# A graph network's edge sums: bf16 parts in threes on 96 rows, or float32r parts in pairs on two 64-row halves

## The chip, the cores and the metric

The kernel runs on one core of a Trainium2 chip. A core has a matrix engine (TensorE, PE in the profile, with its weight loads as PEld), a vector engine (VectorE, DVE), a scalar engine (ScalarE, ACT), a general engine (GpSimd, POOL) and a queue that issues most of the DMA transfers (SyncE, SP). Matrix products go to PSUM, a small memory of eight banks; VectorE and ScalarE read them there. The metric is the time of one execution on the device, in microseconds, as the median of several runs.

## The reference

There are 128 graphs of 128 nodes with 64 features, and an adjacency matrix for each. Layer 0 passes messages over edges, layer 1 is one aggregation.

```python
# layer 0, h = max(layernorm(x), 0)
mask = (adj > 0.0)
xj_proj = h @ W1a
diff = h[:, :, None, :] - h[:, None, :, :]
hid = relu(xj_proj[:, :, None, :] + diff @ W1b + b1)     # (b, j, k, 192)
hm = einsum('bjkh,bjk->bjh', hid, mask)
deg = sum(mask, axis=-1)
x = x + hm @ W2 + deg[..., None] * b2
# layer 1, h = max(layernorm(x), 0)
x = x + einsum('bnm,bmf->bnf', adj, h) @ W.T
```

Only the entries of `mask` that are one add to `hm`. A node has about 16 neighbours among 128 nodes, so most of the (j, k) pairs need not be computed.

## The kernel before

For a node j the hidden vector of an edge to k is relu(A[j] - C[k]), where A = h(W1a + W1b) + b1 and C = h W1b. A and C are 192 wide: units 0 to 127 (C0 = 128) go one way, units 128 to 191 (C1 = 64) another.

**Slots.** The kernel takes the graphs in 32 groups (NG) of four (G = 4). The 128 neighbours k of a node fall into four quarters (Q = 4) of 32. Within a quarter each edge gets a rank, and the first six (D = 6) edges of each quarter go into slots. `pre_rank` (line 442) makes the ranks by a product of a triangular matrix with the mask; `pre_slots` (line 455) compares the ranks with a constant tile `rks` and so makes a one-hot tensor `S`, in bf16. A product of the one-hot tensor with the C values of that quarter picks the neighbour's C for each slot, a product of an identity with the A values adds A[j]. The result lies in PSUM with hidden units on partitions and slot times node on columns. Edges past the sixth of a quarter go an extra way (the `pre_edge_...` functions, `edge_x`, the one-hot tensors `R` and `S2`), and `edge_sum` and `edge_sum1` add what slots and extra edges have in common.

**Exact parts.** TensorE multiplies bf16 in one pass. To keep float32 accuracy the A and C values (`ca`) are split into three bf16 parts in `pre_proj` (line 538): ScalarE copies the product out as the first part, VectorE subtracts it (`rest`), ScalarE makes the second part, GpSimd the third. With 32 nodes of a quarter in three parts, 96 rows (K3) of the array are in use. `pre_stack` (line 607) copies the parts into this layout (`k3`) by 12 transfers, and `pre_slots` copies `S` three times below itself for each quarter (`S3`) by another 12. All of these stand on SP's queue.

**Jobs.** A group has 24 jobs (class `Job`, line 811). A job takes one PSUM tile of two banks; each bank holds one quarter, six slots, 64 nodes (384 columns). A kind-0 job fills all 128 partitions with units 0 to 127 of one graph: two products of 384 columns with `S3` and four of 192 columns with the identity `id3`. A kind-1 job fills two halves of 64 partitions with units 128 to 191 of two graphs: four products of 384 and eight of 192 columns. A kind-0 tile is drained by one VectorE reduction of absolute values into `hm0`; a kind-1 tile by a ScalarE relu into `T` and adds on GpSimd. There are 16 kind-0 and 8 kind-1 jobs in a group, and three tiles of this kind, which `pre_proj` uses too.

**Order.** TensorE's order is the order of the program (`mm` and `tp`, lines 180 to 184). After each job the loop at line 977 runs what three tables name for that step: `AHEAD` prepares the next group, `OWN` belongs to this one, `BEHIND` finishes the group before. The other engines' instructions are placed by the scheduler once the first group has been prepared (`Engine.held`, line 972). The first group has its own preparation: `first_ranks` and `first_slots` make the ranks and slots on tripled rows directly, so that no copies of `S` are needed.

Of the kernel before, what the change touches and what calls it, by code (L numbers as in the profile page):

```python
# [8 lines left out]
F32 = mybir.dt.float32  # L9
BF16 = mybir.dt.bfloat16  # L10
I32 = mybir.dt.int32
# [139 lines left out]
def kernel(  # L151
# [50 lines left out]

    vec, act, pool, sp = (Engine(e) for e in (nc.vector, nc.scalar, nc.gpsimd, nc.sync))
# [15 lines left out]
    K3 = 3 * QN  # L219
# [8 lines left out]
    with ExitStack() as main:  # L228
# [41 lines left out]
        triq = const.tile([P, P], BF16, tag="triq", name="triq")  # L270
        vec.memset(triq, 0.0)
# [3 lines left out]

        triq3 = tmp.tile([P, Q, 3, QN], BF16, tag="u0", name="triq3", bufs=1)
        for part in range(3):
            vec.tensor_copy(
                triq3[:, :, part], triq.rearrange("p (q j) -> p q j", q=Q)
            )  # L280
# [5 lines left out]

        rks = const.tile([P, D, G * N], BF16, tag="rks", name="rks")
        for i in range(D):
            pool.memset(rks[:, i], float(i) + BIG)

        mident = const.tile([P, P], F32, tag="mident", name="mident")
        identb = const.tile([P, P], BF16, tag="identb", name="identb")

        id32 = const.tile([P, QN], F32, tag="id32", name="id32")
        id3 = const.tile([P, QN], BF16, tag="id3", name="id3")
# [3 lines left out]
        def constants():  # L299
            vec.tensor_scalar(mident, ident, -1.0, None, ALU.mult)  # L300
            vec.tensor_copy(identb, ident)
# [3 lines left out]
            vec.tensor_copy(id3, id32)  # L305
# [15 lines left out]

        def weight_loads():
            act.dma_start(w2a, W2[0:C0, :])
            act.dma_start(b1c, b1[0:C0].unsqueeze(1))
            act.dma_start(bias[:, 0:H], b1.unsqueeze(0).to_broadcast([P, H]))
            act.dma_start(b2s, b2.unsqueeze(0).to_broadcast([P, O]))
            for p in range(2):
                s = slice(p * F, (p + 1) * F)
                sp.dma_start(w1[s], W1.rearrange("(t f) h -> f t h", t=2))
# [16 lines left out]
        def weights_b():  # L346
# [3 lines left out]
            pw = mtile("pw")  # L350
            tp(pw[:, 0:P], wab[:, 0:C0], ident)
            vec.tensor_tensor(bias[:, H : H + O], pb[:, 0:O], b2s, ALU.add)
            vec.tensor_scalar(wp[:, 0:H], w1[:, 1], -1.0, None, ALU.mult)
            vec.tensor_copy(wT, pw[:, 0:P])
# [27 lines left out]
        groups: dict[int, dict] = {}  # L382

# [31 lines left out]
        def load(g):  # L415
# [3 lines left out]
            d["adj"] = loads.tile([P, G, N], F32, tag="adj", name=f"adj{g}")  # L419
            sp.dma_start(d["adj"], adj[g * G : (g + 1) * G].rearrange("b j k -> j b k"))  # L420

        def pre_adj(g):
# [8 lines left out]
            d["maskT"] = grp.tile([P, G, N], BF16, tag="maskT", name=f"maskT{g}")  # L431
# [10 lines left out]
        def pre_rank(g):  # L442
# [5 lines left out]
            d["qs"] = grp.tile([P, G, N], BF16, tag="qs", name=f"qs{g}")  # L448
            qf = d["qs"].rearrange("k b j -> k (b j)")
            act.activation(qf, pq, AF.Copy)  # L450

            d["ov"] = grp.tile([P, G, N], BF16, tag="ov", name=f"ov{g}")
            vec.tensor_scalar(d["ov"], d["qs"], float(D) + BIG, None, ALU.is_ge)

        def pre_slots(g, first, last):

            d = groups[g]
            if first == 0:
                d["S"] = one.tile([P, D, G * N], BF16, tag="S", name=f"S{g}")
            n = last - first  # L460
            vec.tensor_tensor(
                d["S"][:, first:last], bc(d["qs"].rearrange("k b j -> k (b j)"), n, 1),
                rks[:, first:last], ALU.is_equal,
            )
            if last < D:
                return
            d["S3"] = grp.tile([K3, Q, D, G * N], BF16, tag="S3", name=f"S3{g}")
            for q in range(Q):
                for part in range(3):
                    sp.dma_start(  # L470
                        d["S3"][part * QN : (part + 1) * QN, q],
                        d["S"][q * QN : (q + 1) * QN],
                    )

        def first_ranks(g, qp):

            d = groups[g]
            pk = gtile(f"pk{g}_{qp}")
            if qp == 0:
                d["q3"] = tmp.tile([K3, Q, G * N], BF16, tag="T", name=f"q3{g}", bufs=3)  # L480
            for i in range(2):
# [545 lines left out]
```

## Time and profile before

| what | us |
|---|---|
| median of three runs | 1012.33 (1009.71 to 1015.56) |
| the profiled execution, its span | 1013.2 |
| busy: PE, DVE, ACT, POOL | 963.8, 799.7, 704.1, 765.9 |
| first job begins | 26.2 |
| groups 1 to 30 | 65.5 to 971.2 |
| last job ends, about | 996 |

The page of the profile has one execution, and this one took as long as the runs. Engines are in rows by their short names. A row of the groups gives line, engine, operation, what is written and read, shapes and count, then busy time, the mean duration of one in ns, and the idle time before such instructions with what ended it. Lines 181 and 184 are the helpers that record each product and transpose, and line 198 the helper that records each instruction of the other engines, so the names of the tiles tell which one is meant. The 40 digits of PEclk are the granted clock of TensorE in tenths, for 40 equal slices of the span.

### The profile page before, as it was taken

What the parts mean: (1) busy time and instruction counts of PE and PEld (TensorE: products, weight loads), DVE (VectorE), ACT (ScalarE), POOL (GpSimd) and SP (SyncE); (2) the same over time, 40 slices, a digit from 0 to 9 for tenths busy, and PEclk for the clock granted to TensorE, in tenths of its full rate; (3) what the DMA queues carried; (4) which work ended last, traced back from release to release, by engine and by line L of the source; (5) the groups of instructions that cost most, each with busy time, mean ns of one, the idle gap of its engine ahead of it and who ended that gap; (6) DMA issues with size and microseconds to landing.
All of it is one profiled execution on the core that took longest, in us unless ns stands there. A gap on an engine that the chain in (4) does not pass through costs nothing.

```text
span 1013.2 us, 27270 instructions
## 1 busy us (share of the span) xinstructions
PE 963.8 (95%) x10314; PEld 721.6 (71%) x10314; DVE 799.7 (79%) x1769; ACT 704.1 (69%) x1732; POOL 765.9 (76%) x1134
## 2 busy tenths in 40 slices
PE   3899999999999999999999999999999999999996
PEld 2577777777777777777777777777767777777774
DVE  7767888777888877788877788877787877788863
ACT  5557876677777667777667787667786667787652
POOL 3278777787877777877778877777877778877783
PEclk9599999999999999999999999999999999999998
DMA  3526655556755556766555766545765555765420
GB/s 83 133 68 162 147 135 130 123 124 154 161 136 134 122 120 140 163 136 138 126 123 129 162 144 136 131 112 128 162 140 133 127 120 132 162 147 119 110 67 14
DMA packets 88296, 129.94 MB, mean 128 GB/s; under 512 B 47200, under 2 KB 63968, under 8 KB 88160
## 3 DMA queue, kind: packets, MB, share of 16 engines
q1 hardware_dynamic: 87584, 127.98, 55.2%
q8 instruction: 83, 1.36, 0.5%
q14 instruction: 53, 0.43, 0.1%
q10 hardware_dynamic: 576, 0.16, 0.1%
HBM read 13.01 MB, written 4.19 MB: 17 GB/s over the span
## 4 chain that ended last, share of the span: by engine, by line
PE 45%; DVE 25%; ACT 14%; DMA 5%; POOL 4%; issue 3%; SPq 2%; DVEq 1%; POOLq 0%; ACTq 0%
PE g L181 24%; DVE hm L198 9%; PE pe L181 8%; DVE S L198 8%; DMA k<-ca 4%; ACT ca L198 3%; PE px L181 3%; DVE u L198 3%; ACT et L198 3%; POOL T L198 3%; SPq L198 2%; PE pp L181 2%; PE py L181 2%; ACT h L198 2%; ACT T L198 2%
## 5 line engine op out<-in xcount | busy, mean ns | idle before, releaser
L198 POOL TENSOR_TENSOR T<-T 128x192 f32<-128x192 f32 (+2 forms) x768 | 543.6, 714 | 139.0 <-ACT T L198 99.1
L181 PEld LDWEIGHTS <-k 96*128 96x128 bf16 (+1 forms) x6144 | 412.4, 104 | 208.5 <-issue 87.4
L198 DVE TENSOR_REDUCE hm<-g 128x64 f32<-128x768 f32 x512 | 472.1, 948 | 110.4 <-PE g L181 108.6
L181 PE MATMUL g<-S,k 96*128 96x384 bf16 (+1 forms) x2048 | 392.1, 333 | 29.2 <-DMA k<-ca 14.3
L181 PE MATMUL g<-id,k 96*128 96x192 bf16 (+1 forms) x4096 | 384.1, 248 | 0.0
L198 ACT ACTIVATE T<-g 128x768 f32<-128x768 f32 x256 | 209.8, 821 | 48.5 <-PE g L181 48.5
L198 POOL TENSOR_TENSOR ca<-rest,ca 128x384 bf16<-128x384 f32 x126 | 114.0, 924 | 82.3 <-ACT ca L198 72.0
L198 ACT ACTIVATE ca<-pp 128x768 bf16<-128x768 f32 x64 | 51.3, 802 | 63.9 <-PE pp L181 63.9
L198 DVE TENSOR_TENSOR S<-qs,rks 128x1024 bf16<-128x1024 bf16 x93 | 86.9, 962 | 0.1
L198 ACT ACTIVATE hT<-ph 128x256 f32<-128x256 f32 x32 | 12.3, 383 | 104.0 <-PE ph L184 104.0
L181 PE MATMUL pe<-RT,X 128*64 128x128 f32 (+1 forms) x512 | 74.9, 285 | 0.0
L181 PE MATMUL pe<-mident,z 128*64 128x128 f32 (+1 forms) x512 | 68.8, 274 | 0.0
L181 PE MATMUL pp<-wp,hT 64*128 64x448 f32 x256 | 68.7, 614 | 0.0
L198 ACT ACTIVATE z<-pp,ns 128x128 f32<-128x128 f32 (+1 forms) x256 | 65.7, 347 | 0.0
L198 ACT ACTIVATE ca<-rest 128x768 bf16<-128x768 f32 x64 | 55.2, 863 | 11.6 <-DVE rest L198 11.6
L198 DVE TENSOR_TENSOR rest<-pp,ca 128x768 f32<-128x768 f32 x64 | 60.7, 948 | 3.2 <-ACT ca L198 3.1
L198 DVE TENSOR_SCALAR maskT<-adjT 128x512 bf16<-128x512 f32 x32 | 17.2, 538 | 52.7 <-PE pe L181 52.7
L198 ACT ACTIVATE et<-et,half 128x128 f32<-128x128 f32 x128 | 56.8, 449 | 0.0
L181 PEld LDWEIGHTS pe<-mident,z 128*64 128x64 f32 (+1 forms) x512 | 53.8, 164 | 0.0
L181 PEld LDWEIGHTS pe<-RT,X 128*64 128x64 f32 (+1 forms) x512 | 52.8, 164 | 0.1
L181 PE MATMUL px<-ca,S 128*128 128x192 bf16 x384 | 52.7, 246 | 0.0
L181 PE MATMUL px<-ca,R 128*128 128x192 bf16 x384 | 52.6, 246 | 0.0
(128 smaller groups left out, 1263.1 us busy)
## 6 DMA issues: line engine op xcount, KB each, us to landing
S<-S SPq DMA_DIRECT2D x372, 192.0 KB, 4.0
k<-ca SPq DMA_DIRECT2D x384, 96.0 KB, 2.2
adj<-in_adj_dram SPq DMA_DIRECT2D x32, 256.0 KB, 3.0
x<-in_x_dram SPq DMA_DIRECT2D x32, 128.0 KB, 2.7
out_dram<-ot SPq DMA_DIRECT2D x32, 128.0 KB, 2.2
w<-in_L_gnn_W_dram SPq DMA_DIRECT2D x2, 96.0 KB, 5.1
bias<-in_L_gnn_b_dram ACTq DMA_DIRECT2D x1, 96.0 KB, 4.6
w2a<-in_L_gnn_W_dram ACTq DMA_DIRECT2D x1, 32.0 KB, 2.2
```

The costliest lines, as they stand in the source:

```text
L181: return tc.keep_in_program_order(nc.tensor.matmul(*args, **kw))
L198: ins = f(*args, **kw)
```

## The change

The A and C values are split into two parts of float32r, a 4-byte type[...], instead of three of bf16. The first part is a ScalarE copy, the second a VectorE subtraction straight from PSUM. 32 nodes in two parts are 64 rows, so that two quarters lie on the two halves of the array: bank 0 of a slot tile is fed by rows 0 to 63, bank 1 by rows 64 to 127. The kind-1 jobs now write all 128 partitions at once; zeros beside the C values keep the halves apart. The ranks are made by two more products on doubled rows, so `S` is made in its final layout by six instructions with a constant, and is copied nowhere. `rks` and the functions for the first group's ranks go away. The mask, the one-hot tensors and the identity become float32r as well. The bodies of `pre_proj` and `pre_stack` follow; the tables are moved to later steps in places, `edge_sum` is cut in two, and some VectorE instructions are now held in the order of the program (`keep`).

```diff
+    def keep(ins):
+        return ins if Engine.held else tc.keep_in_program_order(ins)
...
-            d["adj"] = loads.tile([P, G, N], F32, tag="adj", name=f"adj{g}")
+            d["adj"] = loads.tile([P, G, N], F32, tag="adj", name=f"adj{g}", bufs=1)
...
-            d["maskT"] = grp.tile([P, G, N], BF16, tag="maskT", name=f"maskT{g}")
+            d["maskT"] = grp.tile([P, G, N], F32R, tag="maskT", name=f"maskT{g}")
...
+            pk = gtile(f"pk{g}")
+            for c in range(2):
+                mm(
+                    pk[:, c], trist[:, c], d["maskT"].rearrange("k b j -> k (b j)"),
+                    start=True, stop=True,
+                )
+            d["q2"] = tmp.tile([P, 2, G * N], BF16, tag="q2", name=f"q2{g}", bufs=1)
+            act.activation(d["q2"], pk, AF.Copy)
...
-            vec.tensor_tensor(
-                d["S"][:, first:last], bc(d["qs"].rearrange("k b j -> k (b j)"), n, 1),
-                rks[:, first:last], ALU.is_equal,
-            )
-            if last < D:
-                return
-            d["S3"] = grp.tile([K3, Q, D, G * N], BF16, tag="S3", name=f"S3{g}")
-            for q in range(Q):
-                for part in range(3):
-                    sp.dma_start(
-                        d["S3"][part * QN : (part + 1) * QN, q],
-                        d["S"][q * QN : (q + 1) * QN],
-                    )
+                d["S"] = grp.tile([P, 2, D, G * N], F32R, tag="S", name=f"S{g}")
+            for i in range(first, last):
+                keep(vec.tensor_scalar(
+                    d["S"][:, :, i], d["q2"], float(i) + BIG, None, ALU.is_equal
+                ))
...
-            act.activation(parts[0], x, AF.Copy)
-            rest = tmp.tile([P, 2, 2, H], F32, tag="rest", name=f"rest{g}_{r}")
+            for t in range(2):
+                act.activation(part(0, t), x[:, :, t], AF.Copy)
...
             zs()
             es()
-            vec.tensor_tensor(rest, x, parts[0], ALU.subtract)
-            second()
-            third(pool)
+            for t in range(2):
+                keep(vec.tensor_tensor(part(1, t), x[:, :, t], part(0, t), ALU.subtract))
...
-                sp.dma_start(
-                    d["k3"][part * QN : (part + 1) * QN, q],
-                    d["ca"][q * QN : (q + 1) * QN, part],
-                )
+            for h in range(2):
+                for part in range(2):
+                    for i in range(2):
+                        sp.dma_start(kc[rows(2 * i + part), h], ca[rows(2 * h + i), part])
+                for w in range(2 * h, 2 * h + 2):
+                    for part in range(2):
+                        for i in range(2):
+                            sp.dma_start(ka[rows(2 * i + part), w], ar[rows(w), part])
...
+                if self.kind == 0:
+                    nodes, centre = [(b, p * (H + 2 * C1))], p * (H + C1)
                 else:
+                    nodes, centre = [(r, LOWER), (2 + r, UPPER)], C0
+                for n, (src, a) in enumerate(nodes):
+                    j0 = src * N + jh * JH
+                    for i, rows in enumerate(TILE):
                         mm(
+                            self.gt[:, i, 0:ND].rearrange("h (d j) -> h d j", d=D),
+                            d["kc"][rows, qp, r, a : a + P],
+                            d["S"][rows, qp, :, j0 : j0 + JH],
+                            start=n == 0, stop=False, skip_group_check=True,
                         )
                 for w in range(2):
+                    for i, rows in enumerate(TILE):
+                        o = self.gt[:, i, 0:ND].rearrange("h (d j) -> h d j", d=D)
+                        mm(
+                            o[:, :, w * QN : (w + 1) * QN],
+                            d["ka"][rows, 2 * jh + w, r, centre : centre + P],
+                            bc(id32r[rows], D, 1),
+                            start=False, stop=w == 1, skip_group_check=True,
+                        )
...
-            0: (pre_adj,),
-            2: (pre_norm, pre_hT,),
-            3: (pre_rank, lambda g: pre_slots(g, 0, 2),),
-            4: (lambda g: pre_slots(g, 2, 4),),
-            5: (pre_count,),
-            6: (lambda g: pre_slots(g, 4, D),),
-            7: (lambda g: pre_proj(g, 0),),
-            9: (pre_edge_a,),
-            12: (lambda g: pre_proj(g, 1), pre_stack,),
+            3: (pre_rank,),
+            4: (pre_count, lambda g: pre_slots(g, 0, 1)),
+            6: (lambda g: pre_slots(g, 1, 2),),
+            7: (lambda g: pre_proj(g, 0),),
+            8: (lambda g: pre_slots(g, 2, 3), pre_edge_a),
+            10: (lambda g: pre_slots(g, 3, 4),),
+            11: (lambda g: pre_proj(g, 1), pre_stack),
+            12: (lambda g: pre_slots(g, 4, 5),),
+            14: (lambda g: pre_slots(g, 5, D),),
...
-            1: (edge_sum,),
-            4: (edge_sum1,),
-            8: (post0,),
-            10: (post1,),
+            1: (lambda g: edge_sum(g, 0),),
+            2: (lambda g: edge_sum(g, 1),),
+            5: (edge_sum1,),
+            9: (post0,),
+            13: (post1,),
```

`TILE` is the two row ranges 0 to 63 and 64 to 127, `trist` the triangular matrix with each quarter's columns twice, `kc` the stacked C values with zeros beside them, `ka` the stacked A values. In `edge_x`, `edge_sum` and the extra edges' products the parts are two instead of three.

## The prediction

> **What bounds the kernel now.** I read the page's first part, then the busy time of each engine over one group of the middle of the run, then TensorE's instructions in order of time there, then the groups of VectorE that the change touches.
>
> ```profile
> PE 963.8 (95%) x10314; PEld 721.6 (71%) x10314; DVE 799.7 (79%) x1769; ACT 704.1 (69%) x1732; POOL 765.9 (76%) x1134
> PEclk9599999999999999999999999999999999999998
> 486.60:516.50 29.90, 29.49 (x325) 22.22 (x323) 24.40 (x54) 21.68 (x55) 23.75 (x36) 1.00 0.60 136
> ```
>
> The last line is one group of four nodesets: length, then busy us of PE, weight loads, DVE, ACT, POOL, then the granted clock. PE is busy 29.49 of 29.90. A matmul's record is longer than its turn, so I check by starts:
>
> ```profile
> 499.75 0.66 PE g L181 x6
> 501.59 1.54 PE g L181 x18
> 505.64 0.99 PE px L181 x12
> 486.61 0.60 PE L184 MATMUL pt<-ident,adj 128*128 128x128 f32 x4
> 487.05 0.64 PE L181 MATMUL g<-S,k 96*128 96x384 bf16 x2
> 488.50 0.44 PE L181 MATMUL pe<-RT,X 128*128 128x128 f32 x2
> 488.77 0.39 PE L181 MATMUL pe<-mident,z 128*128 128x128 f32 x2
> 489.00 0.33 PE L181 MATMUL pe<-maskT,ca 128*128 128x128 bf16 x3
> 489.17 0.44 PE L181 MATMUL pe<-RT,X 128*128 128x128 f32 x2
> 503.05 1.02 PE L181 MATMUL pp<-wp,hT 64*128 64x448 f32 x4
> 503.91 0.28 PE L181 MATMUL pp<-biasp,oneb 64*128 64x256 bf16 x2
> 504.17 0.32 PE L181 MATMUL g<-S,k 96*128 96x384 bf16 x1
> ```
>
> The first three are from the chain of waits (start, us, what): a kind-0 job (6 matmuls, 1536 columns) takes 0.66 us, 0.43 ns a column; 12+6 matmuls take 1.54, so a kind-1 job with its switch of array shape about 0.8. The rest is PE's timeline. Three bf16 matmuls of 128 columns take 0.17 us from 489.00 to 489.17 (0.055 each); a plain f32 one of two records 0.23 to 0.27; an f32 transpose, one record, 0.11. PE has no gap to give: it paces the 30 middle groups, which begin at 65.5 us and every 30.2 us to 971.2. The rest is 65.5 us of start with group 0, 24.8 of last group (971.2 to 996.0, PE 24.78 busy) and 17.2 of tail: 65.5+30x30.2+24.8+17.2 = 1013.5, the profiled execution's 1013.2. The median of the runs, 1012.33, is the same within 0.1%.
>
> **The change, TensorE.** Per group there are 16 kind-0 and 8 kind-1 jobs. The trace has no float32r, so its rate is bounded: below by bf16 (0.43 ns a column), above by plain f32 (0.25 us for 128 columns, 1.95 ns), between them the transpose (0.86). The Trainium skill, "FP8 and Floating Point Precision", TensorE Precision Notes, has four passes for true FP32 and a truncating read for reduced precision; that points to one pass, the lower end, which I take. That the two 64-row halves run side by side is seen: the four pp records (two instructions of 448 f32 columns) take 503.91-503.05 = 0.86 us, where one after the other they would take 2x448x1.95 = 1.75.
> - Kind 0: one S pair (384 columns, 0.163) and two id pairs (2x192, 0.081 each): 0.325 instead of 0.65; 16 x -0.325 = -5.2 us.
> - Kind 1: two S pairs, two id pairs: 0.49 instead of 0.78; 8 x -0.29 = -2.3.
> - Three parts become two: px 16 instead of 24 matmuls of 0.083: -0.66; ca with maskT 8 instead of 12 of 0.055: -0.22. The doubled ranks add two of 512 columns: +0.43.
> - Against it, drains. "TensorEngine Tiling (Array Packing)", Key Properties: a change of tiling mode drains the array. Row: the bias pair starts at 503.91 and needs 0.11, the next S matmul, full shape, starts at 504.17: 0.15 idle. Now that is paid around kind 1 and pp; after it, all jobs are half-height and about 16 pieces between them (pt, edge sums, px, py ...) full. I take 0.2 for going and coming, 16 x 0.2 = +3.2. Without the rule it would be nothing.
>
> Sum -4.75: PE needs about 25.4 us a group. A second rule speaks against it: "TensorE: Matmul & The Clock Gate", LDWEIGHTS and Weight-path perf modes: fast weight load is not for FP32, and a load takes columns/1.2, 107 ns for 128. Row: a load of k (128 columns, bf16) reads 98 ns, of the f32 transposes 143, of the f32 products 191. If a 128-column float32r load holds its half for 107 ns, each matmul of 192 or 128 columns costs 0.107: jobs +1.25, px +0.4, maskT +0.4, prt and pgq +0.4, counts +0.2, so 28.1 us. Range 25.4 to 28.1, either below today's 30.2.
>
> **VectorE becomes the pace.** It is busy 24.40 us a group now.
>
> ```profile
> L198 DVE TENSOR_REDUCE hm<-g 128x64 f32<-128x768 f32 x512 | 472.1, 948 | 110.4 <-PE g L181 108.6
> L198 DVE TENSOR_TENSOR S<-qs,rks 128x1024 bf16<-128x1024 bf16 x93 | 86.9, 962 | 0.1
> L198 DVE TENSOR_TENSOR rest<-pp,ca 128x768 f32<-128x768 f32 x64 | 60.7, 948 | 3.2 <-ACT ca L198 3.1
> L198 DVE TENSOR_SCALAR maskT<-adjT 128x512 bf16<-128x512 f32 x32 | 17.2, 538 | 52.7 <-PE pe L181 52.7
> ```
>
> - The 16 reductions stay: 15 us.
> - S: out go three of 962 ns (86.9/31 = -2.8). In come six tensor_scalars of 1024 elements from bf16 to float32r. Nearest row: maskT, also of mixed types and from SBUF, 512 elements, shortest 409 and median 478 ns; two elements a cycle are 0.27 of them, some 0.15 is fixed (ov, 512 bf16, 281 ns): 1024 take 0.53+0.16 = 0.69. S and maskT today also wait: S reads 0.68 when free and 1.48 behind a long POOL add. POOL is busy 70% of the time; I add 0.25 each, half of a mean POOL instruction: 6x0.94 = +5.6. Ends: 4.1 without waits, 7.3 at one element a cycle (6x1.22).
> - rest: two of 948 become four of half size (0.40+0.15): +0.3.
> 27.5 us busy. Some waits cannot be hidden: now S2 waits 0.66 us a group for pgq (21.1 over 32), and ov, dn, ns each wait on the other engines once; I add 1.5: **29.0 us**; with PE at 25 to 28 beside it and three PSUM slots shared by jobs, pp and the new pk, 29.2.
>
> **The others** are covered by VectorE's 29: ACT 21.68 - 2x0.86 (second parts) - 2x0.80 + 4x0.49 (half-size copies, between its 0.42 for 256 and 0.60 for 512) + 1.0 (doubled ranks, 1010 ns in group 0's row) = 21.3. POOL loses four of 0.92: 20.1. SP issues 24 copies a group as now (12 S and 12 k; then 8 kc and 16 ka) at 0.6: 14.2 us. They start when the second pre_proj's remainders are done, some 16.5 us into the group; the first twelve serve the next group's first job and land at 16.5+7.1+2.2 = 26, three us before it; the last are needed six jobs later. Behind them on SP stand only the output and loads for later groups. The one adj buffer is refilled a group ahead. If that cover of 3 us goes, each us late is 30 us in all.
>
> **Start and end.** First job 26.2 now. It loses 8.2 us of S work on VectorE (four of 2.0) and the third parts (1.7), gains six S (4.1), and waits for 12 copies instead of 6 (+3.6): about 27. Group 0 took 39.3, half of it at half clock; with jobs half as long on PE, 37. Together 64. The last group falls from 24.8 to 20.5, where POOL's 19 us of adds and slot sums bound it; tail 17.2. Sum 64 + 30x29.2 + 20.5 + 17.2 = **978 us**.
>
> **Rivals.**
> 1. VectorE costs more: S at one element a cycle or behind every POOL add (+1.7), remainders waiting behind ACT with reductions queued behind them. 31 us a group: 102+930 = 1032. For it: S has been seen at 1.48. Against: maskT's 409.
> 2. The other side: float32r streams at the transposes' rate (0.86 ns a column), or the two halves do not overlap, so the change doesn't do what it says. Kind 0 stays 0.65, kind 1 0.98 (+1.6), drains +3.2, px +0.6, ranks +1.1, the 128-column ones +0.7: PE 37.4, about 1220 us. It turns slower than before as soon as a job's pair takes over 1.5 times its bf16 time. For it: every 4-byte record here takes two cycles or more a column. Against: the precision notes, and pp's halves side by side.
> 3. Only the narrow ones (192 and 128 columns) fall to plain f32's 1.95 ns: kind 0 0.9, kind 1 1.07, px +3.9: PE 45, about 1430.
>
> **Numbers.** My forecast 0.62, its own range 945 to 1020; rival 1 0.11, rival 2 0.17, rival 3 0.10. 0.5% is about what a measurement here can tell from no change. Of my forecast three quarters lie under 1007, and some near it, since PE at 28 and VectorE at 29 may trip over each other: faster 0.62x0.75+0.01 = 0.47; same 0.08; slower 0.45. The range leaves out rival 3 and the best ends: 946 to 1235.
>
> **What would show it.** Right: g<-S records near 326 ns with pairs starting together, PE's busy share falling well below 95% or its idle time naming DVE; S rows of 0.7 to 1.0 us; hm idle time no longer on PE g; groups 29 us apart. Wrong: id pairs more than 0.12 apart (rival 2 or 3), PE still at 95%; S rows above 1.2; PE waiting for ka or adj.

## The result, and the profile after

The changed kernel takes 1515.2 us (median of four runs, 1496.27 to 1539.7) where the kernel before takes 1013.94 (1009.71 to 1015.86). Two of the four ran slower, at a granted clock of 0.70 for 0.73, and the comparison leaves them out: with 1496.27 and 1502.73 us the changed kernel takes 1.481 times as long, 95% interval 1.472 to 1.490. The prediction was 978 us, with a range from 946 to 1235; the result lies outside. The profile below is that of the run of 1502.73 us.

First the page of the changed kernel: busy times, the granted clock in 40 slices, and the groups of jobs, slots and remainders.

```profile
PE 1300.6 (87%) x8967; PEld 1054.0 (70%) x8967; DVE 871.8 (58%) x1927; ACT 699.4 (47%) x1762; POOL 670.5 (45%) x1004
PEclk9888979777778667765777667765677657776688
L182 PE MATMUL g<-S,kc 64*128 64x384 f32 x2048 | 476.4, 504 | 160.3 <-DVE ar L199 71.8
L182 PE MATMUL g<-id32r,ka 64*128 64x192 f32 x3072 | 358.1, 317 | 2.8 <-DMA ka<-ar 2.6
L199 DVE TENSOR_REDUCE hm<-g 128x64 f32<-128x768 f32 x512 | 485.6, 951 | 267.8 <-PE g L182 264.9
L199 DVE TENSOR_SCALAR S<-q 128x1024 fp32r<-128x1024 bf16 x192 | 157.5, 822 | 0.0
L199 DVE TENSOR_TENSOR ca<-pp,ca 128x384 fp32r<-128x384 f32 x64 | 35.7, 558 | 116.6 <-ACT e L199 116.6
```

The second line is what the reader should see first. Before, its digits were nearly all 9; now most are 5 to 8. The mean granted clock of the profiled execution is 0.729 (0.980 before). VectorE, which the prediction made the pace, is busy 58%.

One group in the middle (it begins at 700.7 us and the next at 748.5), in stretches of 5 us: the stretch, its length, then busy us of PE, weight loads, VectorE, ScalarE and GpSimd with counts, then the granted clock and the transfers.

```profile
700.00:705.00 5.00, 5.00 (x27) 4.33 (x27) 2.44 (x3) 0.60 (x1) 3.13 (x6) 0.50 0.19 52
705.00:710.00 5.00, 5.00 (x26) 4.38 (x26) 1.54 (x3) 0.21 (x1) 0.00 (x0) 0.50 0.00 0
710.00:715.00 5.00, 5.00 (x49) 4.10 (x47) 2.76 (x8) 3.15 (x5) 1.08 (x1) 0.83 0.00 0
715.00:720.00 5.00, 4.11 (x43) 2.73 (x40) 3.79 (x8) 3.02 (x12) 4.17 (x7) 1.00 0.02 3
725.00:730.00 5.00, 2.69 (x21) 2.38 (x20) 3.79 (x6) 1.18 (x6) 3.34 (x6) 0.87 0.53 119
740.00:745.00 5.00, 5.00 (x27) 4.08 (x27) 2.34 (x3) 1.19 (x2) 3.33 (x7) 0.50 0.51 116
```

From 700 to 710 TensorE is busy all the time, yet at half clock: 26 or 27 matmuls in 5 us, 49 in the stretch in which the clock comes back. It falls again after the line at 725. The clock changes at steps of 3.413 us, and most groups have settled at exactly 14 of these, 47.8 us: nine at half clock, five at full. The wait that precedes the fall, in TensorE's order of time:

```profile
724.64 0.44 PE L185 MATMUL pty<-ident,ys 128*128 128x128 f32 x2
727.38 0.44 PE L182 MATMUL g<-S,kc 64*128 64x384 f32 x2 [2.31 <-DVE ar L199]
726.21 0.56 DVE L199 TENSOR_TENSOR ca<-pp,ca 128x384 fp32r<-128x384 f32 x1 [2.87 <-ACT e L199]
```

A job waits 2.31 us for its PSUM tile. It is the tile that the projection `pp` held, and the last to read it is the new subtraction `ar`. This one stands on VectorE behind `ca`, and `ca` waits 2.87 us for ScalarE's `e`, though it needs nothing of `e`.

To place the loss, I cut each group in two by the first matmul of `po` (slot 20) and that of `pp` (slot 7 of the next group). Stretch A runs from `po` to `pp`, with slots 21 to 23 and 0 to 7; stretch B from `pp` to `po`, with slots 8 to 20. One group of the kernel before (A, then B), and one of the changed kernel (B, then A):

```profile
572.02:586.61 14.59, 14.55 (x175) 11.85 (x173) 11.99 (x19) 8.43 (x17) 11.48 (x18) 1.00 0.37 89
586.61:601.91 15.30, 14.81 (x151) 10.44 (x151) 12.62 (x37) 13.43 (x38) 12.45 (x19) 1.00 0.82 184
```

```profile
716.07:740.06 23.99, 18.78 (x137) 14.36 (x133) 17.11 (x42) 14.90 (x45) 11.27 (x17) 0.76 0.41 92
740.06:763.86 23.80, 23.80 (x151) 20.29 (x150) 9.84 (x18) 6.94 (x10) 9.71 (x16) 0.59 0.15 36
```

The medians over 27 groups are A 14.86 and B 15.20 before, A 23.80 and B 23.99 after. Both stretches lose about 9 us, but they look different: in A TensorE is never idle and the clock is 0.59; in B TensorE has 5 us without work, and VectorE's busy time has grown by 4.5 us.

### The profile page after: what moved, and what is told of

Its sections match the earlier page's. It is cut to its first block, busy times and chain, and to the rows that moved or that the text cites. A ratio compares the mean times of both kernels' runs of the same rounds, so it can differ in the third digit from the quotient of the medians.

```text
span 1501.0 us, 25137 instructions
## 1 busy us (share of the span) xinstructions
PE 1300.6 (87%) x8967; PEld 1054.0 (70%) x8967; DVE 871.8 (58%) x1927; ACT 699.4 (47%) x1762; POOL 670.5 (45%) x1004
## 4 chain that ended last, share of the span: by engine, by line
PE 56%; DVE 21%; ACT 18%; issue 3%; DMA 1%; POOL 1%; ACTq 0%; DVEq 0%; SPq 0%; POOLq 0%
PE g L182 23%; PE pe L182 12%; DVE hm L199 9%; ACT h L199 5%; DVE S L199 5%; PE pp L182 5%; ACT z L199 4%; ACT T L199 3%; PE po L182 2%; DVE ar L199 2%; PE prt L182 2%; PE pt L185 2%; PE pgq L182 2%; ACT ar L199 2%; PE pj L182 2%
## 5 line engine op out<-in xcount | busy, mean ns | idle before, releaser
L199 POOL TENSOR_TENSOR T<-T 128x384 f32<-128x384 f32 (+2 forms) x640 | 484.4, 763 | 738.5 <-ACT T L199 708.3
L182 PE MATMUL g<-S,kc 64*128 64x384 f32 x2048 | 476.4, 504 | 160.3 <-DVE ar L199 71.8
L182 PEld LDWEIGHTS g<-S,kc 64*128 64x128 f32 x2048 | 223.9, 236 | 302.2 <-issue 110.6
L182 PEld LDWEIGHTS g<-id32r,ka 64*128 64x128 f32 x3072 | 385.7, 251 | 3.9 <-issue 2.0
L182 PE MATMUL g<-id32r,ka 64*128 64x192 f32 x3072 | 358.1, 317 | 2.8 <-DMA ka<-ar 2.6
L199 DVE TENSOR_SCALAR S<-q 128x1024 fp32r<-128x1024 bf16 x192 | 157.5, 822 | 0.0
L199 POOL TENSOR_TENSOR T<-T,T 128x192 f32<-128x192 f32 x128 | 75.5, 590 | 10.0
L182 PE MATMUL pe<-maskT,ca 128*128 128x128 f32 x256 | 77.9, 401 | 0.0
L182 PE MATMUL px<-ca,S 128*128 128x192 f32 x256 | 71.6, 371 | 0.0
L182 PE MATMUL px<-ar,R 128*128 128x192 f32 x256 | 69.6, 366 | 0.0
```

Of the source, the lines that this page charges most:

```text
L182: return tc.keep_in_program_order(nc.tensor.matmul(*args, **kw))
L199: ins = f(*args, **kw)
```

## Experiments

Each of the kernels below was run once, beside the kernel before (1011 to 1018 us). The changed kernel's own four runs lie 2.9% apart, so a difference of under three per cent between its variants is not read. The row "changed" is its profiled run, with which the others are compared. "Group" is the mean distance of the group starts from group 1 to group 30.

| kernel | us | clock | group, us |
|---|---|---|---|
| before | 1013.9 | 0.980 | 30.2 |
| changed | 1502.7 | 0.729 | 46.3 |
| e1_fill: 10 dense matmuls ahead of `pty` | 1357.0 | 0.900 | 41.4 |
| e2_px: `edge_x` at slots 12 and 13 | 1532.4 | 0.73 | 47.6 |
| e3_dense: one dense pair in each job | 1394.1 | 0.943 | 42.7 |
| e4_fill2: fill behind `pty` and in slot 17 | 1486.0 | 0.845 | 45.6 |
| e5_early: subtractions ahead of `z`, `e` | 1372.5 | 0.802 | 42.0 |
| e6_before_gap: the kernel before with a gap | 1236.6 | 0.898 | 37.6 |
| e8_burst: three bursts | 1390.5 | 0.885 | 42.6 |
| e9_early_burst: e5 with bursts | 1337.6 | 0.887 | 40.9 |
| e10_et: e5 with `et` later | 1425.7 | 0.768 | 44.1 |
| e11_et_burst: e10 with bursts | 1334.7 | 0.912 | 41.0 |
| e12_slate: e5 with four `S` blocks later | 1271.3 | 0.852 | 38.6 |
| e13_slate_burst: e12 with bursts | 1283.0 | 0.903 | 39.0 |

### Is it float32r, the gap, or the thin stream?

The first theory, A, was that an idle gap throttles the clock and that the new stream is too thin to bring it back. A kernel of streams only and three edits of the changed kernel tried it. The streams (the bodies of the functions are told in words here): 96-row bf16 jobs, float32r jobs back to back, float32r jobs with four full-height bf16 matmuls behind each, plain float32, and combinations, parted by rests of 13 or 3 us.

```python
def job64(t):                 # float32r: t = sr; bf16: t = sb
    # S pair of 384 columns, then two id pairs of 192, on the two halves
def full(n):                  # n bf16 matmuls, 128 rows, 128 columns
```

> All of the kernel's work is left out; TensorE runs streams of matmuls one after the other, each after a rest of some 14 us, and the granted clock is read in each: 70 bf16 jobs on 96 rows (384,384,4x192 columns) as before; 110 float32r jobs on two halves; 80 of those with four full-height bf16 matmuls of 128 columns after each; 200 plain f32 ones of 128 columns; 60 float32r jobs with two S pairs; bf16 jobs with gaps of about 3 us; then three times 100 bf16 matmuls of 512 columns, 40 float32r jobs, a 3 us gap, 40 jobs with full-height pieces. Theory A (a gap throttles, and the mixed float32r stream is too thin to end it): the bf16 stream comes to full clock within 10 us and falls for a while after a 3 us gap; the float32r stream with full-height pieces stays at 0.5 to its end when it starts cold, and keeps 1.0 when it follows dense matmuls without a gap. Rival B (the thin stream throttles by itself, no gap needed): the float32r jobs right behind the dense stretch fall to 0.5 within some 20 us. Rival C (the clock follows busy time alone): every stream that keeps TensorE busy comes to 1.0 within 10 us. At full clock a kind-0 float32r job takes 0.40 us back to back and 0.50 with pieces between.

Measured (787.26 us in all), stretches of 10 us of the streams kernel: stretch, length, busy PE, weight loads, VectorE, GpSimd, clock, transfers.

```profile
90.00:100.00 10.00, 10.00 (x156) 10.00 (x154) 0.00 (x0) 0.00 (x0) 1.00 0.01 2
200.00:210.00 10.00, 10.00 (x70) 7.51 (x66) 0.00 (x0) 0.00 (x0) 0.50 0.01 2
290.00:300.00 10.00, 10.00 (x92) 10.00 (x91) 0.00 (x0) 0.00 (x0) 1.00 0.01 2
```

The first is float32r jobs alone, at full clock 4.2 us after their start; the third plain float32. The second is the float32r job with four full-height pieces: TensorE is busy 10.00 of 10.00 us, and the clock stays at half for all of the 123 us of this stream. So rival C falls: being busy does not bring the clock back, and float32r alone is no hindrance. This stream also settles the rate that two rivals of the prediction were about: the records of the two halves start 2 to 7 ns apart, and a kind-0 job has 0.20 us for its S pair and 0.20 for its two id pairs.

The edits, all in the changed kernel: `e1_fill` has ten 512-column bf16 products ahead of `pty`, overwritten by it; `e2_px` moves a step; `e3_dense` gives each job a pair of 512-column products that its own then overwrite.

```diff
 e1   +            for i in range(10):
      +                mm(pt, oneb, dmy, start=True, stop=True)
 e2   -            14: (lambda g: edge_x(g, 0),),
      -            16: (lambda g: edge_x(g, 1),),
      +            12: (lambda g: edge_x(g, 0),),
      +            13: (lambda g: edge_x(g, 1),),
 e3   +                for i, rows in enumerate(TILE):
      +                    mm(self.gt[:, i], oneb[rows], dmy[rows], start=True, stop=True)
```

> The changed kernel with ten dense bf16 matmuls of 512 columns (their result is overwritten) in front of the pty transposes, where TensorE stands 2.6 us in each group. Theory A (the gap starts the half clock): mean clock from 0.73 to over 0.95, groups of 32 to 33 us, about 1090 us in spite of 2.1 us more work a group. Rival B (the thin stream throttles by itself): clock stays under 0.8 and groups at 46 us or more, 1450 us or more. Rival C (the float32r matmuls' own cost, clock or not): 1515 us plus up to 64.

> The changed kernel with the two px pieces moved from steps 14 and 16 to 12 and 13, so that 2.4 us of useful work stands where TensorE waits for pp's slot. Theory A: the 2.6 us gap shrinks under 1 us, the clock stays over 0.95 and groups come to 30 to 32 us, 1010 to 1070 us. Rival B: the clock stays under 0.8, about 1450 us. Rival C: 1515 us, as the work is the same.

> The changed kernel with one pair of dense bf16 matmuls of 512 columns on the two halves ahead of each job's own (overwritten by them): 24 x 0.213 = 5.1 us more work a group at full clock, the gap stays. Theory A: the clock still falls after the gap but returns sooner, mean clock 0.8 to 0.9, groups of 38 to 42 us, 1250 to 1350 us. Rival B: the stream is now dense enough, clock over 0.95, groups 35 to 36 us, about 1170 us. Rival C: 5.1 us a group dearer at least, 1670 us or more.

`e1_fill` filled the gap and was 146 us faster for it, though it does more work, but far from the 1090 us expected: a new wait of 3.4 us appeared four slots later, behind a norm of which VectorE and ScalarE make parts in turn, and the clock fell there. `e2_px` left gaps of 1.78 and 1.33 us and the same 47.8 us groups: a miss. `e3_dense` had the clock nearly full,

```profile
PEclk8899999999999999999999999999999999999998
```

and yet its groups took 42.7 us, above the 35 to 42 expected, of which the pairs themselves take about 5. So the clock is a large part of the loss, not the whole.

### What brings the clock back

> A measurement of its own: all of the kernel's work is left out; TensorE streams in stretches parted by rests of about 13 us, looked at by the granted clock. Theory A (a gap sets the clock to half, and a stream that alternates between half-height pairs and full-height pieces is too thin to set it back, because of the alternation itself): the float32r job plus four full-height pieces stays at half clock after a rest, and so does the same with bf16 half-height jobs and with float32r full-height pieces; full-height float32r alternating with full-height bf16, and the 96-row bf16 job plus four full pieces as in the kernel before, are at full clock within 2 windows of 3.4 us; directly behind 60 dense 512-column matmuls, with no gap, the alternation keeps the full clock. Rival T (it is the mix of float32r and bf16, not the two heights): bf16 half-height jobs with full pieces warm up, full-height float32r with bf16 stays at half. Rival B (the thin stream throttles by itself): behind dense matmuls with no gap it falls to half within 3 windows. Three jobs to twelve or to four full pieces show how many switches it takes; no theory has a number for them. Two short rests at the end (about 0.5 and 1.7 us) show which gap is still harmless.

Measured, the streams of this kernel in the order of the text above: float32r job and full bf16 pieces directly behind dense matmuls; then, each after a rest, the same with bf16 half-height jobs, with float32r full pieces, full-height float32r and bf16 in turn, the 96-row job with full pieces, three jobs to twelve pieces. Three jobs to four pieces, not shown, came back to full clock too.

```profile
75.00:85.00 10.00, 10.00 (x112) 7.76 (x114) 0.00 (x0) 0.00 (x0) 1.00 0.01 2
125.00:135.00 10.00, 10.00 (x134) 5.71 (x132) 0.00 (x0) 0.00 (x0) 1.00 0.01 2
220.00:230.00 10.00, 10.00 (x51) 8.55 (x51) 0.00 (x0) 0.00 (x0) 0.50 0.00 0
340.00:350.00 10.00, 10.00 (x64) 10.00 (x63) 0.00 (x0) 0.00 (x0) 0.50 0.01 2
425.00:435.00 10.00, 10.00 (x117) 8.49 (x115) 0.00 (x0) 0.00 (x0) 1.00 0.01 2
490.00:500.00 10.00, 10.00 (x141) 9.07 (x138) 0.00 (x0) 0.00 (x0) 1.00 0.01 2
```

Theory A was wrong about the cause: alternating heights does warm up in bf16 (line 2), and full-height float32r with bf16 does not (line 4), so it is not the change of heights. Rival T was no better: three jobs to twelve pieces mix the types and warm up (line 6). And the thin stream does not fall by itself when it starts at full clock (line 1), against rival B.

What orders all of these is the share of time in which columns stream. I worked it out from the traces: each matmul's columns (twice for a plain float32 record), at 0.42 ns each at full clock (512-column ones start 0.216 us apart) and twice that at half, products on both halves counted once, over each step of 3.41 us. It is an estimate: some records are missing from a trace, and another way of counting records that overlap moves most steps by up to 0.06 and one in the table below (718.5) by 0.12. At half clock lines 3 and 4 stream 0.48 to 0.56 and 0.61 to 0.69 of the time. The streams here that came back had 0.78 or more in the step before. The low values go with the weight loads: float32r pieces of 128 columns start 0.11 us apart, of which 0.053 is columns, so they stream 48% of their time; bf16 pieces start 0.055 apart. Pieces of 64 columns among the float32r ones do not change the distance (92 starts in 10 us in each of the first three lines of the next section), and weight loads are busy 10.00 of 10.00 us there. That the clock follows the share is theory D. In the changed kernel's group above:

| step starts at, us | 701.4 | 704.8 | 708.2 | 711.7 | 715.1 | 718.5 | 721.9 | 725.3 | 728.7 | 732.1 | 735.6 |
|---|---|---|---|---|---|---|---|---|---|---|---|
| clock | 0.5 | 0.5 | 0.5 | 1 | 1 | 1 | 1 | 1 | 0.5 | 0.5 | 0.5 |
| streamed share | 0.75 | 0.72 | 0.77 | 0.59 | 0.53 | 0.74 | 0.57 | 0.29 | 0.70 | 0.70 | 0.44 |

Over the whole changed kernel, a step at full clock that was followed by half had a share of 0.20 to 0.42; one followed by full 0.40 or more. At half clock, steps followed by full had 0.73 to 0.95, steps followed by half up to 0.78. The kernel before streams 0.88 (median) at full clock. Three more kernels:

```diff
 e4   +            for i in range(18):                  # behind pty's transposes
      +                mm(pt[:, 256:512], oneb, dmy[:, 0:256], start=True, stop=True)
      +                for k in range(10 if self.t == 17 else 0):   # dense pairs as in e3
 e5   +            for t in range(2):
      +                keep(vec.tensor_tensor(part(1, t), x[:, :, t], part(0, t), ALU.subtract))
                   zs()
                   es()
      -            for t in range(2):
      -                keep(vec.tensor_tensor(part(1, t), x[:, :, t], part(0, t), ALU.subtract))
 e6   +            mm(pt[:, 0:4], upb, gb, start=True, stop=True)
      +            (nine ScalarE copies, the first from pt, the last to gb)
      +            mm(pt[:, 0:4], upb, gb, start=True, stop=True)
```

> The changed kernel with overwritten dense bf16 matmuls in two places of each group: 18 of 256 columns behind the transposes of post1 (about 2 us at full clock) and 10 pairs of 512 columns ahead of the job in slot 17 (about 2.2 us), so that neither of the two long waits of TensorE is an idle one; nothing else changed, the output is the same. Theory A (the clock is what is lost): clock 0.95 or more from the second group on, groups of 33 to 37 us (29.0 of TensorE's work at full clock, 3.4 of stalls, up to 4.2 of fill that is not hidden), 1060 to 1190 us. Rival R (the waits themselves are the loss, the clock only fills them): groups stay at 40 us or more with the clock full, over 1280 us. If the gap only moves again, as with one fill: 41 us groups and a mean clock near 0.9.

> The changed kernel with one edit: in the projection the two subtractions that make the second float32r parts are issued ahead of the scaled copies z and e, so that VectorE waits for ScalarE's two copies only and no longer for the six instructions behind them (0.93 + 0.42 us by the trace of the changed kernel). Theory A: TensorE's longest gap in each group shrinks from 2.58 to about 1.2 us; if that is too short to set the clock to half, groups fall to 31 to 34 us and the time to 1020 to 1110 us. Rival R (waits count at face value): 2 x 1.35 us less in each group at most, groups of 45 us, 1420 us. If the remaining gap still throttles, the group stays at 14 windows of 3.4 us, 47.8 us, and the time at 1500.

> The kernel before with one TensorE gap of about 2.5 us made in each of groups 1 to 30, at slot 11: a tiny matmul whose right operand is made by a chain of nine tiny ScalarE copies from the result of another tiny matmul; all else as before, the output is the same. Theory A (the stream of the kernel before is dense enough to recover): the clock falls to half for one or two windows of 3.4 us in each group, so groups of 30.2 + 2.5 + 1.7 to 3.4 us = 34.4 to 36.1, 1140 to 1195 us. Rival G (any such gap costs what it cost the changed kernel, nine windows at half): groups of 43 us or more, 1400 us. If the gap does not throttle at all: 32.7 us, 1090 us.

`e4_fill2` missed: no wait in its groups lasts over 1.4 us, but several fall into one step, whose share is then 0.32 to 0.43, and the clock falls anyway. It is the sum over a step that counts, not the longest wait. `e5_early` gained 130 us, more than its face value (45 us groups) and less than hoped. All of it is the clock in stretch A, whose mean falls from 22.6 to 18.0 us; B stays at 24. `e6_before_gap` made gaps of 4.8 us, not 2.5, since the tiny copies stood behind ScalarE's other work; what follows the gap is what matters:

```profile
571.00:576.00 5.00, 1.46 (x13) 0.86 (x12) 1.58 (x12) 5.00 (x23) 1.81 (x3) 0.81 0.98 216
576.00:581.00 5.00, 5.00 (x22) 2.44 (x21) 1.00 (x2) 3.03 (x9) 2.81 (x5) 0.51 0.22 46
581.00:586.00 5.00, 5.00 (x68) 4.37 (x66) 3.51 (x4) 3.41 (x11) 2.13 (x3) 1.00 0.43 98
```

Two steps at half clock, then full again, in nearly every group, at shares of 0.76 and 0.92. The bf16 stream pays for a gap twice as long with 7.4 us a group, where the changed kernel stays at half for nine steps.

### The limits of the share

> A measurement of its own: all of the kernel's work is left out. Theory D, formed from the runs so far: the clock of a window of 3.4 us follows from the share of the window before in which TensorE streams columns (columns of the matmuls x 0.417 ns at full clock, 0.833 at half, over the window), not from its being busy: at half clock a share above about 0.75 sets the clock to full, at full clock a share under about 0.40 sets it to half, in between it stays. Float32r pieces of 128 columns stream for 48% of their time[...]. TensorE has no gap inside the stretches here. Five stretches behind a rest, of float32r pieces (128 columns) and bf16 matmuls of 512 columns in the ratios 8:3, 2:1, 5:3, 3:2 and 4:3, streamed shares about 0.70, 0.74, 0.76, 0.78 and 0.79 at half clock: D expects the first to stay at half to its end, the last two to be at full within 3 windows, and the limit between. Five stretches directly behind 60 dense matmuls at full clock: float32r pieces of 128 columns alone (0.48), with one of 64 columns to four (0.44), to two (0.40), to one (0.37), and 64-column ones alone (0.25): D expects the first to stay full and the last two to fall to half though TensorE is never idle. Rival I (only an idle gap sets the clock to half): all five stay full. Rival C (busy is enough): all of the first five warm up.

Measured, the five stretches behind dense matmuls, shares 0.48, 0.44, 0.40, 0.37 and 0.25:

```profile
190.00:200.00 10.00, 10.00 (x92) 10.00 (x91) 0.00 (x0) 0.00 (x0) 1.00 0.00 0
230.00:240.00 10.00, 10.00 (x92) 10.00 (x92) 0.00 (x0) 0.00 (x0) 1.00 0.01 2
270.00:280.00 10.00, 10.00 (x92) 10.00 (x91) 0.00 (x0) 0.00 (x0) 1.00 0.01 2
320.00:330.00 10.00, 10.00 (x49) 10.00 (x49) 0.00 (x0) 0.00 (x0) 0.50 0.00 0
390.00:400.00 10.00, 10.00 (x49) 10.00 (x48) 0.00 (x0) 0.00 (x0) 0.50 0.00 0
```

All five look equally busy. The first three have 92 matmuls in 10 us at full clock; the last two fall to half after one step, with no gap at all. Every product has its weight load in all five, so what differs is the columns. That is theory D's lower limit, between 0.37 and 0.40, and it refutes rival I. The upper limit was a miss: the 8:3 stretch also came back to full. At half clock it repeats every 2.91 us, of which 2.13 are columns, a share of 0.73. The stream in `m1_streams` that stays at half repeats every 1.53 us with 1.07 of columns, a share of 0.70, and the changed kernel stayed at half in steps of up to 0.78. So my count is not exactly what the chip counts, and the upper limit is known only as some 0.70 to 0.78. The Trainium skill, "TensorE: Matmul & The Clock Gate", Part 1 (The HAM clock gate), has half clock after an idle window and full after a busy one; these runs show both directions to depend on streamed columns while TensorE is busy throughout, and the measurement decides.

### What holds the group at 41 us with the clock up

```diff
      +                for k in range({16: 4, 20: 4, 0: 4}.get(self.t, 0)):   # dense pairs as in e3
```

> The changed kernel with three bursts of four overwritten pairs of 512-column bf16 matmuls in each group, ahead of the jobs in slots 16, 20 and 0, in the stretch that ran at half clock; nothing is done about the waits, the output is the same. Each burst is 0.85 us of streaming at full clock, 1.7 at half. Theory D: after the fall at the wait in slot 14 a burst lifts a window from a share of 0.64 to 0.75 to over 0.77 and sets the clock back, so that 2 to 4 windows of a group run at half and no longer 9: groups of 32.4 (full-clock equivalent of the changed kernel's group) + 2.6 (bursts) + 3.4 to 6.8 = 38.4 to 41.8 us, 1225 to 1330 us, against 1515 although work is added. Rival R (the waits of the engines set the pace): the group stays at 44 us or more, over 1390 us.

> The same bursts in the kernel with the subtractions issued early (e5_early, 1372 us). Theory D: groups of 31 to 33 + 2.6 + 1.7 to 5.1 us = 36 to 40 us, 1150 to 1280 us. Rival R: not under e5_early's 1372 us, since the bursts only add work.

The bursts worked on the clock: in `e8_burst` a fall lasts about two steps instead of nine, 1390 us for 1503 with work added. But both kernels missed theory D's times by 60 us: with the clock at 0.89 groups still take 41 to 43 us. Two stretches, once more, tell why. This is `e5_early`, first an A at full clock, then the B ahead of it:

```profile
691.56:706.77 15.21, 15.21 (x150) 12.98 (x150) 9.47 (x18) 6.72 (x10) 10.07 (x16) 1.00 0.23 56
667.60:691.56 23.96, 18.64 (x136) 14.40 (x132) 16.42 (x42) 15.09 (x45) 10.75 (x17) 0.79 0.41 92
```

With the clock full, stretch A takes 15.20 us (median of 12 such groups), about what it took before (14.86). Of A's 8.9 us, 8.6 are the clock. Stretch B is another matter. In eight settled groups of `e4_fill2` the clock is full in all of it, and B still takes 24.5 us:

```profile
1237.37:1261.90 24.53, 18.84 (x175) 13.72 (x172) 17.20 (x42) 14.90 (x45) 10.89 (x17) 1.00 0.38 87
```

TensorE has 5.7 us without work there, although up to 4.1 us of its busy time is fill. If none of the fill hid in waits, B would take 20.4 us without it, against 15.2 before.

In `e9_early_burst`, the chain of waits through B (start, us, what) runs over VectorE and ScalarE:

```profile
941.87 0.54 DVE ca L199
942.41 0.46 DVE ar L199
942.87 0.86 DVE hm L199
943.73 0.60 DVE S L199
...
944.50 1.28 ACT et L199 x4
...
945.96 1.26 ACT et L199 x4
947.22 1.39 ACT T L199 x2
948.61 0.38 ACT ca L199
...
949.39 0.56 DVE ca L199
949.95 0.47 DVE ar L199
950.41 0.86 DVE hm L199
951.28 0.60 DVE S L199
```

Both `ca` and `ar` have to wait for ScalarE, which does `et` first, and the reductions `hm` that free TensorE's tiles stand behind them. Two theories of what to take out, each with and without bursts: `et` (eight ScalarE instructions, moved to slot 12, behind the second projection), then four of six `S` blocks.

```diff
 e10  -                act.activation(d["et"][:, b, :], iov, AF.Abs, bias=mid[:, b : b + 1])
      ...                                        # its eight instructions go into pre_et
      +            12: (lambda g: pre_slots(g, 4, 5), pre_et),
 e12  -            8: (lambda g: pre_slots(g, 2, 3), pre_edge_a),
      -            10: (lambda g: pre_slots(g, 3, 4),),
      -            12: (lambda g: pre_slots(g, 4, 5),),
      -            14: (lambda g: pre_slots(g, 5, D),),
      +            8: (pre_edge_a,),
      +            17: (lambda g: pre_slots(g, 2, 3),),
      +            18: (lambda g: pre_slots(g, 3, 4),),
      +            20: (pre_place, lambda g: pre_slots(g, 4, 5)),
      +            22: (lambda g: pre_slots(g, 5, D),),
```

> The kernel with the early subtractions (e5_early) with one more edit: the eight ScalarE instructions that make et are issued in slot 12 and in that order, behind the second projection's copies; in the changed kernel they run ahead of them. Theory Q (at full clock the group is paced by a chain of ScalarE's and VectorE's queues between slots 8 and 18, in which each instruction waits for the one ahead in its engine's order): the chain of e9_early_burst has et twice, 1.28 + 1.26 us, between VectorE's mid and ScalarE's second ca copy; they leave the path, and groups are 2.5 us shorter, 40.5 on the mean for 43.0, 1290 us for 1372; less if the shorter wait also keeps the share of streaming over 0.40 and with it the clock, down to 36 us, 1150 us. Rival D alone (only the clock matters): 1340 to 1372 us, no less than with the bursts.

> The same with the three bursts of e8_burst and e9_early_burst, which keep the clock near full. Theory Q: groups of 40.7 - 2.5 = 38.2 us, 1260 us against e9's 1337.6. Rival D alone: unchanged at 40.7 us and 1338 us, as the clock was at 0.887 of full already.

> The kernel with the early subtractions (e5_early) and four of the six S blocks made later: in slots 17, 18, 20 and 22 for 8, 10, 12 and 14, so that VectorE does them while TensorE sets the pace and not between slots 8 and 18. Theory Q2 (the group is the sum of two stretches with different limits: slots 18 to 8 of TensorE's work at full clock, slots 8 to 18 of a chain on VectorE and ScalarE, in which S blocks, hm and the projection's parts follow one another): the chain of e11_et_burst has S in that stretch with 0.60 + 0.96 + 0.60 + 0.60 = 2.8 us and more; groups about 2.8 us shorter, 40.2 us on the mean for 43, 1290 us for 1372; lower (to 36 us, 1150 us) if shorter waits also keep the share of streaming over 0.40. Rival D alone: as e5_early, 1372 us.

> The same with the three bursts of e9_early_burst. Theory Q2: groups of 40.7 - 2.8 = 37.9 us, 1250 us for 1337.6. If the stretch is only moved to another chain, as with et in e11: 40.7 us and 1335.

`et` was a miss: 1334.7 against 1337.6 us. It left the chain, and the chain went on over `S`, `hm`, the statistics and ScalarE's `h` and `X` in nearly the same time. Without bursts it was even slower (1425.7): B is 1.3 us shorter on the mean (22.8 for 24.1), at a higher clock (0.82 for 0.78), but A is 3.3 longer, as the clock stays at half for 6.4 steps a group instead of 5.1. `S` was a hit by its number: 1271.3 us without bursts, where 1290 was expected, 101 us less than `e5_early`, for moving four instructions of 0.7 to 0.9 us within VectorE's order. But by the means B shrinks only from 24.1 us in `e5_early` to 22.6, at about the same clock, which is 1.5 of the 2.8 us expected, and A from 18.0 to 16.0. At full clock A has not become shorter (16.0 for 15.2), so the larger part of the gain is the clock, which now stays up in A. With bursts, which keep it up in A anyway, B falls from 24.9 us in `e9_early_burst` to 22.8 (clock 0.83 in both), and the time is 1283.0, 55 us less and 33 above what was expected. How far B would fall with nothing waiting was not tried; none of these kernels comes near the kernel before.

## Why the prediction was wrong

**The step that failed: TensorE's 25.4 to 28.1 us "either below today's 30.2".** The working took the granted clock of 1.00 from the kernel before and kept it. The change replaces bf16 pieces, in a stream of 0.88, by float32r ones: 128-column products start 0.11 us apart with 0.053 of columns, and a kind-0 job takes 0.40 us with 0.32. That costs little time, but it takes the stream to about 0.6 at full clock and 0.7 at half, so that a few waits within 3.4 us bring the clock down and little brings it up. Stretch A shows it alone: 15.20 us at full clock, 23.80 as it ran.

**TensorE's own sum came out a little over its upper value.** The turns at full clock add up to 29 to 30 us a group (15.2 in stretch A, and in B at most the 18.84 busy us of the line above less 4.1 of fill), where the prediction gave 28.1 with the weight-load rule. The rule pointed the right way: a kind-0 job takes 0.40 us where its columns alone were reckoned at 0.325. Between full-height pieces it takes 0.50 to 0.57, and a kind-1 job up to 0.75 for 0.57, which fits the drains that were reckoned with. But 29 leaves at most 1.2 of the 4.75 us that the first sum gained. In stretch A nothing was gained (15.20 for 14.86).

**"VectorE becomes the pace" failed in its form.** Its busy time was right: 871.8/32 = 27.2 us a group against 27.5, with `S` at 822 ns against 940. But a busy time per group is not a pace. Of VectorE's work 17.1 us lie in stretch B (12.6 before), above all because `S` moved there: 4.1 us of it, where before 2.9 us of `S` were in A. There, with the waits for ScalarE's copies and three tiles for TensorE, B takes at least 20.4 us at full clock instead of 15.2. This is rival 1's "remainders waiting behind ACT with reductions queued behind them", which the prediction had priced at 1.8 us a group.

**The sum.** Of the 17.7 us that a settled group is longer, A's clock is 8.6 and A's work 0.3; of B's 8.8, at least 5.2 are there at full clock too (`e4_fill2`), and at most 3.6 are the clock. That VectorE's and ScalarE's order makes these 5.2 us is shown in part: the move of `S` took 1.5 to 2.1 us out of B at an unchanged clock, the move of `et` none, and the rest was not tried. Chain and clock belong together, as the waits of the chain bring the clock down, and the thin stream keeps it there.

**Start and end.** The first job began at 28.85 us (predicted about 27) and group 1 at 73.7 (64). Of the signs named ahead, `S` rows of 0.7 to 1.0 us came true, and TensorE's busy share fell, to 87%; but the groups are 46.3 us apart and not 29, and `hm` still waits mostly for TensorE.

**The rivals.** Rival 2, by which the range reached 1235, and rival 3, which the range left out, rested on a slow rate of float32r or on halves that do not overlap. The halves do overlap, and the S pair of 384 columns takes 0.20 us at full clock, so neither happened. The right side, with 0.45 on slower, was there for the wrong reason.

## What to carry to other kernels

When an edit makes TensorE's pieces smaller or their weights dearer, work out the share of time in which columns stream, not only the sum of the turns: a stream that falls from 0.9 to 0.6 or 0.7 may not bring back a clock that a few waits have brought down, and each such step costs half its time. Sum busy times by stretch of the loop and not over it, and ask for each moved instruction in which stretch it now stands: four `S` blocks in the wrong slots cost 101 us here, 1.5 us a group in their own stretch and 2 us by the clock in the other. When such a clock has fallen, a longer program can be a faster one (1390 us for 1503, with three bursts of products that are thrown away), which is a test rather than a cure.

## What was not expected of the hardware

- TensorE can be busy 10.00 of 10.00 us and run at half clock for as long as the stream lasts (123 us), and a stream without a gap can fall from full clock to half when its share is 0.37, while one of 0.40 stays.
- The two limits lie far apart: down at about 0.40, up at some 0.70 to 0.78. Between them a stream keeps the clock that it finds. The same float32r jobs with full-height pieces ran at full clock behind dense matmuls and at half behind a rest.
- Groups lock to the steps of the clock: most take 14 steps of 3.413 us, 47.8 us, in the changed kernel, and again in `e2_px`, whose waits differ.
